# Four edits of order in a perceiver layer: scores and values, a weight load, a norm factor, a bank

## The chip, the cores and the metric

The kernel runs on one core of a Trainium2 chip. The metric is the device time of one execution in microseconds (us), as the median of several runs. The profile is one execution recorded by the hardware profiler.

## What is computed

One layer takes x of 256 tokens by 512 and a context of 4096 tokens by 512, all in 32-bit floats, and adds three blocks to x, each on a layernorm of it:

```python
x = x + _L0_xattn_ref(_layernorm(x), ctx_2048, ...)   # attention
x = x + _L0_attn_ref(_layernorm(x), ...)              # state-space block
x = x + _L0_ffn_ref(_layernorm(x), ...)               # mixture of experts
```

The attention has 16 query heads and 4 key heads of 128, RMS norms on queries and keys, a causal part over the tokens themselves and a full part over the context. The state-space block projects its input, runs a causal convolution of length 4, mixes tokens in two chunks of 128 with decays exp(A_cs[i] - A_cs[j]) of running sums per head, carries a state from the first chunk to the second, gates with silu(z), normalizes and projects back. The mixture routes each token to 6 of 32 experts of width 192, weighs their results, and adds a shared expert of width 384.

## The kernel before

Tokens lie in two tiles of 128 (t = 0, 1). The program is written in plain Python, and a planner fixes the order on each engine: it simulates the program with times of its own and takes, of what is ready on an engine, what stands earlier in the program. Every engine then works strictly in that order and waits on semaphores. `tc.issue_after(ins)` adds an edge: what is traced inside comes behind `ins` on the same engine. DMAs are issued by SP (`nc.sync`), by ACT (`nc.scalar`) and by POOL (`nc.gpsimd`), each a queue in order.

**Attention** (`bounded_attention`). Step s = 0 takes the tokens' own keys, steps 1 to NC = 8 one chunk of 512 context keys each. A step is a list of pieces (s, g, t, i): key head g, token tile t, key block i; 12 pieces in step 0, 32 in the others. For each piece `scores` (L567) is a matmul into one of three `sc` banks, ACT takes exp of it (L573) into one of four `prT` tiles, and DVE multiplies the block on the diagonal by a mask (L576) or adds the probabilities up (L583). `values` (L592) multiplies them by the values into `oT`. The program issues the values of a piece two pieces after its scores (`pending`). Beside steps 1 to 7 run the products of the next chunk's keys and values (`fast_steps`, L364), whose keys are transposed by DVE and through DRAM (`turn_heads`: `kd<-tr` L263, `kT<-kd` L265), as are most queries in step 0 (`qT<-qd`). In the last step the key blocks come in the order 1, 3, 2, 0.

**State-space block.** It begins inside the last step. `decays(t)` brings the running sums to all partitions: ACT writes them to DRAM (L844), POOL loads them 128-fold into `lm`, 1 MB (L845); DVE subtracts each head's own sum (L849, 16 instructions) and ACT takes exp (L850, 4). `channels` projects and convolves (L864 to L873), `gates` computes silu(z) (L885), `mixing` multiplies `lm` by the products of B and C (L910), `assemble` gates y (L952 to L962), `turn_y` transposes it (L971, L972) and `mamba_out` projects it back (L978), adds it to x (L979) and calls `layernorm`, whose factor is a power on POOL (`power_half`, L196); L206 then writes xn.

**Mixture.** `route`, `ranks`, `rows_of` give each token's experts and rows (L1004 to L1077). `scatter(t)` issues 6 indirect DMAs from POOL (L1022) that write xn to the experts' rows in DRAM. `shared_hidden` and `shared_down` (L1135 to L1149) are the shared expert. `hold` gives the experts' weights, two experts a pair, the buffers that have come free, and loads the first pairs from SP (L1165, L1166); the later pairs are gathered by POOL (L1158). `Rounds` then runs the pairs of experts: the rows of the first two pairs are picked by a matmul (`ps_pick`, L1466, copied by DVE and ACT at L1468), the others fetched from DRAM.

**Banks of PSUM.** There are 8: `ps_tp` 1, `ps_mm` 2, `ps_sc` 3, `ps_o` 2. `bank(name)` takes the next of a ring over `mm`, `sc` and `tp`. Before `Rounds` these pools close and others take over the banks: `ps_x` 2, `ps_gu` 2, `ps_t` 1, `ps_ye` 3; the first matmul into a bank waits until what lay there has been read.

Of the kernel before, what the change touches and what calls it, by code (L numbers as in the profile page):

```python
# [19 lines left out]
P = 128  # L20
# [53 lines left out]
def perceiver_layer(ctx: ExitStack, tc: tile.TileContext, a: dict, out: bass.AP):  # L74
# [65 lines left out]
    def layer(ctx, bounded):  # L140
# [410 lines left out]
        def bounded_attention(beside):  # L551

            pp = pool("pp", 4)
            bq = small.tile([P, 3], FP, tag="bq", name="bq", bufs=1)
            V.tensor_reduce(bq[:, 0:1], qw_bc, AX.X, ALU.max, apply_absolute_value=True)
            V.tensor_reduce(bq[:, 1:2], kw_bc, AX.X, ALU.max, apply_absolute_value=True)
            shift = bq[:, 2:3]
            V.tensor_scalar(shift, bq[:, 0:1], bq[:, 1:2], -float(np.sqrt(HD)), ALU.mult, ALU.mult)
            V.tensor_scalar(shift, shift, BOUND, None, ALU.add)
            outs, first_pr, masked = {}, [], []  # L560

            def scores(s, g, t, n):

                kT, _, r = kv[s]
                i = keys_of(s, t)[n]
                sc = ps_sc.tile([P, REP * P], FP, tag="sc", name="scT")
                TE.matmul(sc, kT[:, g, i * P:(i + 1) * P], qT[:, t, heads4(g), :].rearrange("p h q -> p (h q)"),  # L567
                          start=True, stop=True)
                la = lacc[:, t, g, :]

                alone = s == 0 and t == 0
                pr = la if alone else pp.tile([P, REP * P], FP, tag="pr", name="prT")
                S.activation(pr, sc, AF.Exp, bias=shift, scale=SCALE if r is None else r[:, i, g:g + 1])  # L573
                if s == 0 and i == t:
                    p3 = pr.rearrange("p (h q) -> p h q", q=P)
                    masked.append(V.tensor_tensor(p3, p3, upper.unsqueeze(1).to_broadcast([P, REP, P]), ALU.mult).ins)  # L576
                if s == 0:
                    if n < t:
                        first_pr.append(pr)
                    elif not alone:  # L580
                        V.tensor_tensor(la, first_pr.pop(), pr, ALU.add)
                else:
                    V.tensor_tensor(la, la, pr, ALU.add)  # L583
                return pr

            def values(s, g, t, n, pr):
                _, v, _ = kv[s]
                keys = keys_of(s, t)
                i, last = keys[n], n == len(keys) - 1
                if n == 0:  # L590
                    outs[g, t] = ps_o.tile([P, REP * P], FP, tag="o", name="oT")
                TE.matmul(outs[g, t], v[:, i, g * HD:(g + 1) * HD], pr, start=(n == 0), stop=last)  # L592
                if last:
                    ov = oacc[:, t, g, :]
                    if s == 0:
                        V.tensor_copy(ov, outs.pop((g, t)))
                    else:
                        V.tensor_tensor(ov, outs.pop((g, t)), ov, ALU.add)  # L598
                    if s == NC:
                        ps = ps_sc.tile([P, REP * P], FP, tag="sc", name="ps_l")  # L600
                        TE.matmul(ps, ones, lacc[:, t, g, :], start=True, stop=True)
                        rl = lacc[:, t, g, :]
                        V.reciprocal(rl, ps)  # L603
                        V.tensor_tensor(aT[:, t, heads4(g), :].rearrange("p h q -> p (h q)"), ov, rl, ALU.mult)

            pending = []
            for s in range(NC + 1):
                if s < NC:
                    steps = [(s, g, t, i) for g in range(NKV) for t in range(NT) for i in range(len(keys_of(s, t)))]
                else:  # L610
                    steps = [(s, g, t, i) for t in range(NT) for g in range(NKV) for i in range(len(keys_of(s, t)))]
                    last_weights()
                extra = []
                if 0 < s < NC:
                    if s + 1 < NC:
                        load_ctx(s + 1)
                    extra = fast_steps(s, heads_done[4] if s == 1 else None)
                    extra.insert(len(extra) // 2, lambda: clear(s - 1))
                done = 0
                for n, st in enumerate(steps):  # L620
                    if s == 0 and n == 3:
                        for turn in turns:
                            turn()
                    if s == 0 and n == 8:
                        with tc.issue_after(masked[-1]):
                            last_sum()
                    pending.append((*st, scores(*st)))
                    if s == 0 and st[3] == len(keys_of(s, st[2])) - 1:
                        q = qT[:, st[2], heads4(st[1]), :]
                        S.activation(q, q, AF.Copy, scale=kw_col)  # L630
                    if len(pending) > 2:
                        values(*pending.pop(0))
                    if s < NC:

                        while done < min(len(extra), len(extra) * (n + 1) // (len(steps) - 4)):
                            extra[done]()
                            done += 1
                    elif n > len(steps) // NT + 1:
                        for f in beside():
                            f()  # L640
            for p in pending:
                values(*p)
# [151 lines left out]
        def steps_of(t):  # L794
# [37 lines left out]
                    S.activation(m["e1", t], acs, AF.Exp)  # L832
            return product, series, sums

        def decays(t):


            lm, acs = m["lm"], m["acs", t]

            def spread_sums():  # L840
                ps = bank("ps_csT")[0:SH, 0:P]
                TE.matmul(ps, m["dA", t], upper, start=True, stop=True)
                S.copy(m["csT", t], ps)
                S.dma_start(sums_d[t], m["csT", t])  # L844
                G.dma_start(lm, sums_d[t].partition_broadcast(P))  # L845

            def piece(q):
                for hh in range(q * 4, q * 4 + 4):
                    V.tensor_scalar(lm[:, hh, :], lm[:, hh, :], acs[:, hh:hh + 1], 0.0, ALU.subtract, ALU.min)  # L849
                S.activation(lm[:, q * 4:q * 4 + 4, :], lm[:, q * 4:q * 4 + 4, :], AF.Exp)  # L850
            return [spread_sums] + [lambda q=q: piece(q) for q in range(4)]

# [122 lines left out]
        def mamba_out(t):  # L975
            ps = bank("ps_out")
            for k in range(DIT):
                TE.matmul(ps, m["yT", t][:, k, :], w_out[k // 4][:, k % 4, :], start=(k == 0), stop=(k == DIT - 1))  # L978
            V.scalar_tensor_tensor(x_sb[:, t, :], ps, m["ry", t], x_sb[:, t, :], ALU.mult, ALU.add)  # L979
            layernorm(t)  # L980


        def routing_memory():
# [32 lines left out]
                            m["idx"][:, t, 0:TOPK].unsqueeze(2).to_broadcast([P, TOPK, NE]), ALU.is_equal)  # L1016
            V.tensor_reduce(m["mask"][:, t, :], m["hot"][:, t].rearrange("p k e -> p e k"), AX.X, ALU.add)

        def scatter(t):

            for k in range(TOPK):
                G.indirect_dma_start(  # L1022
                    out=xg_rows[t * TOPK + k], in_=xn[:, t, :], in_offset=None,
                    out_offset=bass.IndirectOffsetOnAxis(ap=row[:, t, k:k + 1], axis=0))
# [118 lines left out]
            return product, turn  # L1143

        def shared_down(t):
            ps = bank("ps_shared")
            for j in range(FT):
                TE.matmul(ps, m["act"][:, j, tok(t)], sd[:, j, :], start=(j == 0), stop=(j == FT - 1))
            V.tensor_tensor(x_sb[:, t, :], ps, x_sb[:, t, :], ALU.add)  # L1149
# [8 lines left out]
            G.indirect_dma_start(out=out, out_offset=None, in_=src,  # L1158
                                 in_offset=bass.IndirectOffsetOnAxis(ap=place[:, c:c + 1], axis=0))

        def load_weights(to, n, fixed):

            if fixed:
                for i in range(2):
                    nc.sync.dma_start(to[i], a["experts"][2 * n + i])  # L1165
                nc.sync.dma_start(to[2], a["down_rest"][2 * n:2 * n + 2].rearrange("e p n -> (e p) n"))  # L1166
            else:
                s = 2 * n - FIXED
# [1 line left out]
                    rows_at(to[i], a["experts"].rearrange("e p n -> (e p) n"), s + i)  # L1170
                rows_at(to[2], a["down_rest"].rearrange("e p n -> (e p) n"), NE - FIXED + s // 2)

        def load_pair(n):
            if n < NP:
                k = n % NHELD
                weights[n] = (held[2 * k], held[2 * k + 1], rests[k])
                load_weights(weights[n], n, 2 * n < FIXED)

        def hold(*tiles):

            for tl in tiles:
                held.append(carve(tl, (WEX,))[0])
                if len(held) % 2 == 0 and len(held) <= FIXED:
                    load_pair(len(held) // 2 - 1)


        run = lambda fs: [f() for f in fs]
# [51 lines left out]
        sums()  # L1239
        lm[0]()  # L1240
        run(chans[1][c] for c in order[3:])
        hold(*w_x, lacc[:, 0])
        run(gates(0))
        run(lm[1:])
        assemble(0)
        silu[1]()
        run(tokens_back(1))
# [15 lines left out]
        ranks(0)  # L1263
        rows_of(0)
        product, turn = shared_hidden(0)
        mamba_out(1)
        product()
        scatter(0)
        hold(wvc, wkc, ctx0)
        hold(*w_out)  # L1270
        pick = pick.rearrange("p (t e) r -> p t e r", t=NT)
# [366 lines left out]
```

## Time and profile before

| | us |
|---|---|
| median of 3 runs (996.19, 996.37, 998.72) | 996.37 |
| the profiled execution | 998.33 |
| its span, first to last instruction | 996.6 |
| PE busy | 970.6 |
| DVE busy | 499.3 |
| ACT busy | 386.2 |
| POOL busy | 204.8 |
| mean granted clock of PE | 0.996 |

The time of the profiled execution holds its span and 1.7 us around it. PE is TensorE, DVE VectorE, ACT ScalarE, POOL GpSimd and SP the engine that issues DMAs. A matmul of 32-bit floats is recorded as two instructions, 0.43 us apart at 512 columns, so a score or a value takes PE 0.86 us. Times in the views count from the start of the span; a name such as `oT<-prT,v` is what an instruction writes and reads.

### The profile page before, as it was taken

The numbers are of one execution on the slowest core, as the hardware profiler recorded it, in microseconds if no ns is written. First come the engines' busy times: TensorE is split into PE (matmuls) and PEld (weight loads), VectorE is DVE, ScalarE is ACT, GpSimd is POOL, SyncE is SP. The second block draws the span as 40 slices with busy tenths as digits, with TensorE's granted clock in tenths as the row PEclk, the third lists the DMA queues.
The fourth block names the chain that finished last, engine by engine and source line by source line (L and its number), as shares of the span: only waits on it lengthen the run. The fifth ranks groups of instructions, "written<-read, shape, count | busy, mean of one in ns | idle before, by whom it ended". The sixth has DMA issues, their size and how long they took to land.

```text
span 996.6 us, 8898 instructions
## 1 busy us (share of the span) xinstructions
PE 970.6 (97%) x2742; PEld 456.7 (46%) x2742; DVE 499.3 (50%) x999; ACT 386.2 (39%) x851; POOL 204.8 (21%) x212
## 2 busy tenths in 40 slices
PE   7999999999999999999999999999999898999996
PEld 3444444444444444444444444444466554555442
DVE  4456554454453544544545545458596655422134
ACT  3645543443443443434434434343162821122210
POOL 4443001101100201200200200000013324444533
PEclk9999999999999999999999999999999999999998
DMA  8735032213313304304304113140054542899964
GB/s 318 230 74 150 21 97 95 62 33 115 85 21 127 84 6 142 85 0 148 74 11 148 34 32 83 56 115 1 1 183 169 211 177 109 316 343 352 393 231 121
DMA packets 131580, 125.91 MB, mean 126 GB/s; under 512 B 80225, under 2 KB 99586, under 8 KB 126274
## 3 DMA queue, kind: packets, MB, share of 16 engines
q1 hardware_dynamic: 119216, 77.96, 25.9%
q0 software_dynamic: 7984, 41.16, 11.1%
q10 hardware_dynamic: 4322, 6.11, 1.7%
q8 instruction: 24, 0.39, 0.2%
q14 instruction: 34, 0.28, 0.1%
HBM read 89.02 MB, written 36.19 MB: 126 GB/s over the span
## 4 chain that ended last, share of the span: by engine, by line
PE 94%; DMA 2%; DVE 1%; ACT 1%; issue 1%; POOL 1%; SPq 0%; ACTq 0%; DVEq 0%
PE oT L592 23%; PE scT L567 23%; PE ps_kv L364 17%; PE ps_egu L218 5%; PE ps_self L218 3%; PE ps_v L218 2%; PE ps_o L788 2%; PE ps_egu L1373 2%; PE total L1441 2%; PE ps_ye L1450 2%; PE ps_k L218 1%; PE ps_out L978 1%; PE ps_xbc L218 1%; PE xgTp L1354 1%; PE ps_ye L1453 1%; DMA lm<-sums 1%
## 5 line engine op out<-in xcount | busy, mean ns | idle before, releaser
L583 DVE TENSOR_TENSOR lacc<-lacc,prT 128x512 f32<-128x512 f32 x256 | 182.7, 714 | 240.4 <-ACT prT L573 239.6
L573 ACT ACTIVATE prT<-scT,bq,rk 128x512 f32<-128x512 f32 x256 | 198.8, 777 | 255.4 <-PE scT L567 242.7
L567 PE MATMUL scT<-qT,kT 128*128 128x512 f32 x536 | 270.9, 592 | 0.0
L592 PE MATMUL oT<-prT,v 128*128 128x512 f32 x528 | 268.0, 592 | 0.9 <-ACT prT L573 0.9
L592 PEld LDWEIGHTS oT<-prT,v 128*128 128x128 f32 x528 | 100.1, 190 | 127.2 <-issue 115.0
L567 PEld LDWEIGHTS scT<-qT,kT 128*128 128x128 f32 x536 | 101.2, 190 | 124.6 <-issue 121.9
L196 POOL TENSOR_TENSOR rk<-pv,mhalf 128x4 f32<-128x4 f32 x32 | 32.3, 1009 | 371.1 <-DVE pv L195 371.1
L364 PE MATMUL ps_kv<-wkv,fast 128*128 128x512 f32 x112 | 53.4, 592 | 0.0
L254 ACT ACTIVATE sq<-kraw 128x128 f32<-128x128 f32 x128 | 35.7, 279 | 45.2 <-DVE kraw L382 43.2
L364 PE MATMUL ps_kv<-wkv,ctx 128*128 128x512 f32 x112 | 52.8, 592 | 0.0
L364 PE MATMUL ps_kv<-fast,fast 128*128 128x512 f32 x112 | 52.6, 592 | 0.0
L598 DVE TENSOR_TENSOR oacc<-oT,oacc 128x512 f32<-128x512 f32 x64 | 43.7, 682 | 0.0
L364 PEld LDWEIGHTS ps_kv<-wkv,fast 128*128 128x128 f32 x112 | 21.3, 190 | 26.8 <-issue 26.8
L364 PEld LDWEIGHTS ps_kv<-wkv,ctx 128*128 128x128 f32 x112 | 21.3, 190 | 26.8 <-issue 23.7
L364 PEld LDWEIGHTS ps_kv<-fast,fast 128*128 128x128 f32 x112 | 21.3, 190 | 26.8 <-issue 21.8
L358 POOL TENSOR_TENSOR fast<-ctx 128x512 f32<-128x512 f32 x7 | 9.3, 1334 | 113.1 <-PE ps_kv L364 94.2
L382 DVE TENSOR_TENSOR kraw<-ps_kv,fast 128x256 f32<-128x256 f32 x42 | 17.9, 425 | 28.2 <-PE ps_kv L364 28.2
L1425 DVE TENSOR_TENSOR hid<-si,ps_egu 128x128 f32<-128x128 f32 x18 | 5.2, 287 | 53.3 <-ACT si L1423 53.3
L788 PE MATMUL ps_o<-wo,qT 128*128 128x512 f32 x64 | 28.8, 592 | 0.0
L218 PE MATMUL ps_self<-wq,xT 128*128 128x512 f32 x64 | 28.1, 592 | 0.0
L603 DVE RECIPROCAL lacc<-ps_l 128x512 f32<-128x512 f32 x8 | 26.8, 3346 | 0.1
L364 PE MATMUL ps_kv<-fast,ctx 128*128 128x512 f32 x56 | 26.3, 592 | 0.0
(392 smaller groups left out, 1131.6 us busy)
## 6 DMA issues: line engine op xcount, KB each, us to landing
xg<-xn SPq DMA_DIRECT2D x6, 2560.0 KB
ctx<-in_ctxT_dram SPq DMA_DIRECT2D x7, 1024.0 KB
kd<-tr SPq DMA_DIRECT2D x112, 64.0 KB
kT<-kd SPq DMA_DIRECT2D x28, 256.0 KB
ye<-y_sb ACTq DMA_DIRECT2D x22, 256.0 KB
wq<-in_wq_dram SPq DMA_DIRECT2D x4, 1024.0 KB
wo<-in_wo_dram SPq DMA_DIRECT2D x4, 1024.0 KB
w_in<-in_W_inT_dram SPq DMA_DIRECT2D x4, 1024.0 KB
```

Of the source, the lines that this page charges most:

```text
L196: return G.tensor_tensor(dst, v[:, :n], mhalf[:, :n], ALU.pow)
L218: TE.matmul(ps, lhs(k), rhs_of(k), start=(k == 0), stop=(k == KD - 1))
L254: S.activation(sq[:, h, :], raw[:, h, :], AF.Square, accum_out=ss[:, h:h + 1])
L364: TE.matmul(ps, lhs(k), rhs(k), start=(start and k == 0), stop=(k == 1), skip_group_check=True)
L567: TE.matmul(sc, kT[:, g, i * P:(i + 1) * P], qT[:, t, heads4(g), :].rearrange("p h q -> p (h q)"), start=True, stop=True)
L573: S.activation(pr, sc, AF.Exp, bias=shift, scale=SCALE if r is None else r[:, i, g:g + 1])
L583: V.tensor_tensor(la, la, pr, ALU.add)
L592: TE.matmul(outs[g, t], v[:, i, g * HD:(g + 1) * HD], pr, start=(n == 0), stop=last)
L598: V.tensor_tensor(ov, outs.pop((g, t)), ov, ALU.add)
L603: V.reciprocal(rl, ps)
L788: TE.matmul(m["ps_o", t], aT[:, t, h, :], wo[j][:, h % 4, :], start=(h == 0), stop=(h == NH - 1))
L1373: TE.matmul(ps[self.half(i)], xT[:, k, self.half(i)], w[i][:, k, :], start=(k == 0), stop=(k == KD - 1))
```

## The change

Nothing is computed otherwise, and no instruction is added or removed. Four edits change an order or a bank:

1. In step 0, and in the first four pieces of the last step, the values issued after a piece's scores get an edge behind those scores.
2. `hold(*w_x, lacc[:, 0])`, which loads the first pair of experts, moves behind `gates(0)` and the decays, and its two loads of 1 MB wait for the first DVE instruction of the decays of tile 1 (L849), which reads `lm`.
3. `scatter(0)` is cut into 2 and 4 indirect DMAs; the 4 stand behind the norm factor of `layernorm(1)` on POOL.
4. `shared_down(1)` takes a bank of `ps_o` in place of the ring's next.

```diff
+                scored.append(TE.matmul(sc, kT[:, g, i * P:(i + 1) * P], qT[:, t, heads4(g), :].rearrange("p h q -> p (h q)"),
+                                        start=True, stop=True).ins)
...
                     if len(pending) > 2:
-                        values(*pending.pop(0))
+                        with tc.issue_after(scored[-1]) if s == 0 or (s == NC and n < 4) else nullcontext():
+                            values(*pending.pop(0))
...
-                    V.tensor_scalar(lm[:, hh, :], lm[:, hh, :], acs[:, hh:hh + 1], 0.0, ALU.subtract, ALU.min)
+                    begun = V.tensor_scalar(lm[:, hh, :], lm[:, hh, :], acs[:, hh:hh + 1], 0.0, ALU.subtract, ALU.min)
+                    if hh == 0:
+                        decay_begun.append(begun)
...
-            layernorm(t)
+            return layernorm(t)
...
-        def scatter(t):
-            for k in range(TOPK):
+        def scatter(t, ks=range(TOPK)):
+            for k in ks:
...
-            ps = bank("ps_shared")
+            ps = bank("ps_shared") if t == 0 else ps_o.tile([P, REP * P], FP, tag="o", name="ps_shared")
...
+        def wait_for(dma, behind):
+            if behind is not None:
+                tc.add_manual_dep(dma.ins, behind.ins.name, mybir.DependencyInfo(
+                    mybir.DependencyClass.Sync, mybir.DependencyReason.DATA), reason="transfers in order")
...
-                    nc.sync.dma_start(to[i], a["experts"][2 * n + i])
+                    wait_for(nc.sync.dma_start(to[i], a["experts"][2 * n + i]), behind)
...
-        hold(*w_x, lacc[:, 0])
         run(gates(0))
         run(lm[1:])
+        hold(*w_x, lacc[:, 0], behind=decay_begun[-1])
...
-        mamba_out(1)
+        normed = mamba_out(1)
         product()
-        scatter(0)
+        scatter(0, range(2))
+        with tc.issue_after(normed.ins):
+            scatter(0, range(2, TOPK))
```

## The prediction

> **What bounds the kernel now.** I read the page first, then the waits of TensorE, then the chain of waits, and last the timeline around each wait.
>
> ```profile
> span 996.6 us, 8898 instructions
> PE 970.6 (97%) x2742; PEld 456.7 (46%) x2742; DVE 499.3 (50%) x999; ACT 386.2 (39%) x851; POOL 204.8 (21%) x212
> ```
>
> TensorE (PE) is busy for 970.6 of 996.6 us, and the change neither adds nor removes a matmul. Only the 26.0 us in which PE is idle can shrink: 6.3 us wait for the first weights and 7.7 us lie behind the last matmul (it ends at 988.87). Of the rest, the waits of PE from 60 us on are, the longest first:
>
> ```profile
> PE ps_pick L1466 <- DVE x_sb L1149: 1.9, 1, 1.9
> PE ps_out L978 <- DVE qT L972: 1.8, 1, 1.8
> PE ps_sh L1141 <- DVE sh L1136: 1.6, 1, 1.6
> PE oT L592 <- DVE lacc L576: 1.5, 1, 1.5
> PE oT L592 <- ACT prT L573: 0.9, 1, 0.9
> ```
>
> Each is one wait, and each part of the change touches one or two. The two `oT` waits sit at 98.10 us (step 0) and 662.35 us (last step). The chain of waits shows how the 1.8 us at `ps_out` arise:
>
> ```profile
> 777.52 9.31 DMA lm<-sums
> 786.90 1.28 ACT L850
> 788.19 0.63 ACT lm L850
> 788.84 1.28 ACT L885
> 790.13 0.60 ACT wkv L885
> 790.75 1.28 ACT L850
> 792.04 0.64 ACT lm L850
> 792.71 0.69 DVE lm L910
> 793.40 0.61 DVE qT L972
> 794.05 7.13 PE ps_out L978 x16
> ```
>
> The columns are start, length and what ran. The transfer of the running sums (9.31 us) is followed by ScalarE (ACT), which loads a table (1.28 us) at each turn between exp and silu. The windows around `ps_pick` show a second loss:
>
> ```profile
> 842.44:844.30 1.86, 0.00 (x1) 0.00 (x1) 1.70 (x8) 0.00 (x0) 1.55 (x2) 1.00 0.68 262
> 844.30:848.00 3.70, 3.70 (x5) 1.65 (x6) 1.82 (x11) 0.00 (x0) 2.79 (x4) 0.54 0.49 189
> ```
>
> After 1.86 us without a matmul the granted clock (third number from the end) is 0.54 over 3.70 us. That stretch loses 3.70 x 0.46 = 1.70 us. It counts as busy time.
>
> **Part 1, values behind scores.** In step 0 PE runs the scores of piece 6 at 95.58, then at once the values of piece 6, which need exp (0.69) and mask (0.69); hence 1.50 us of wait. With the edge, values 4, 5 and the scores 7, 8 come between: 4 x 0.86 = 3.44 us of work covers the chain. The price would be a score that waits for its query. The last query transfer is issued at 88.38 and its bytes are over by 91.5 us; score 7 then comes at about 95.5, 4 us later. Gain 1.5 us, bounds 0 and 1.6.
> In the last step PE runs three values at 657.84 (2.58 us) while the fourth key block is in flight (issued 657.49, bytes from 658.5 to 660.0), takes its score at 660.41 and waits 0.92 us for its exp. With the edges the second value stands behind that score. If other scores fill the time, 0.92 us are gained. If none does, PE waits from 658.70 to about 660.2, 1.5 us, and saves 0.92 + 0.25 of the old order, so it loses 0.3. Between the ends I take 0.5, nearer to the gain, since the next group's scores need neither that block nor a new query.
>
> **Part 2, weights behind the sums.** Two experts' weights (1 MB each, SP, 777.32) and `lm` (1 MB, POOL, 777.52) share the DMA engines. Between 777 and 782 the hardware queue moves 1.02 MB and POOL's queue 0.25. The same transfer for the other tile, issued at 734.96 with nothing beside it, had its bytes between 736.0 and 739.1, 4.1 us after issue. Alone, `lm` lands at 781.7 instead of 786.8; VectorE (DVE) is ready at 782.50 and drops its 4.35 us wait. What is late next is ACT: its silu ends at 785.85, so its table load moves from 786.90 only to 785.87. The five ACT steps behind it, 5.8 us, stay, then L910 and L972 follow: `ps_out` starts 1.0 us earlier, 0.8 us still waited. Bounds: 0 (next paragraph) and 1.77. The held loads now start at about 783; behind them on SP stand the loads of `lacc` (782.81) and later ones, first read from 858 on, the held ones from 852.97: 60 us of cover, without which 2 MB would cost 5 us.
> The row: POOL's transfer was issued at 777.52 and its bytes came late, while DVE ran short f32 products without a break (777.09 to 782.50). The Trainium skill, "SBUF — State Buffer", section "SBUF: two separate sides", says that a DVE operation holding the shared port keeps GpSimd from writing descriptors, so that such a transfer seems blocked. By that rule the weights are not the cause, and part 2 would be worth 0.0 us instead of 1.0; the transfer of the other tile, 4.1 us with DVE 4.42 of 4.54 us busy, speaks against it.
>
> **Part 3, a norm factor between scatters.** The timeline around 825 us (start, length, engine, line, operation; in brackets the idle time before and what ended it):
>
> ```profile
> 824.03 0.96 POOL L1022 DMA_INDIRECT xg<-xn,row  x1 [0.30 <-issue]
> 825.01 0.59 POOL L196 TENSOR_TENSOR rs<-pv,mhalf 128x1 f32<-128x1 f32 x1
> 825.63 0.61 DVE L206 TENSOR_SCALAR xn<-x_sb,mv,rs 128x512 f32<-128x512 f32 x1 [3.04 <-issue]
> 826.16 0.54 DVE L1136 TENSOR_TENSOR sh<-sh,ps_sgu 128x384 f32<-128x384 f32 x1
> 826.76 0.55 PE L1141 MATMUL ps_sh<-ident,sh 128*128 128x128 f32 x3 [1.64 <-DVE sh L1136]
> ```
>
> The factor's input is ready at 822.6 us, but POOL first issues four scatters (1.27 us each); DVE stands 3.04 us on L206, and L1136 behind it. With two scatters ahead POOL is free at 822.46, the factor is done at 823.4, L206 at 824.05. L1136 then waits for the last `ps_sgu` matmul (825.12) and PE goes on at about 825.8, not 826.76: 1.0 us. Bounds 0.3 (L206 late by half a scatter) and 1.64 (the transposes of xn fill the gap). The four scatters behind end 0.4 us later (828.5 for 828.08); the next on POOL comes at 838.40, so that costs nothing; without that cover, 0.4.
>
> **Part 4, another bank.** `ps_pick` waits for L1149 to read `ps_shared` (844.24), whose bank it takes over. In a bank of `ps_o` that read is off the path: `ps_pick` may start at 842.44. Of the 1.86 us, DVE can take back 1.0: its queue is full until 846.22, the copy of the first quarter stands there, and the third quarter (842.44 + 2 x 1.72 = 845.9) needs that bank, free at 846.9. Bounds 0.86 and 1.86; I take 1.4. The half-rate stretch, 1.7 us, should go with the wait.
> Row: 1.86 us without a matmul, then 3.4 us at half rate. The Trainium skill, "TensorE: Matmul & The Clock Gate", section "What's actually happening", says that the clock falls after an idle window of about 3.4 us, and that windows run free of the kernel. By it so short a wait is not the cause, and the stretch would stay, with a profile at 992.9 in place of 991.2; the trace's length agrees with the window, its cause not.
>
> **Sum.** 1.5 + 0.5 + 1.0 + 1.0 + 1.4 = 5.4 us, 7.1 with the clock. The profiled execution took 998.33 (span 996.6 and 1.7 around it); the runs' median is 996.37, 1.96 lower. That is about the 1.7 us of the stretch, so I take it that the two faster runs had none. Profile: 998.33 - 7.1 = 991.2. Median: 996.37 - 5.4 = 991.0. Behind 853 us PE is busy throughout and carries the gain to the end: the last weights are in at about 957.5 and used at 973, so an earlier PE meets no DMA. I forecast 991.1.
>
> **Rivals.**
> A. The waits form again in the queues of DVE and ACT: last step -0.3, part 2 nothing, part 4 0.86, first step 1.5, part 3 0.3. That gives 2.4 us, 994.0. For it: ACT and DVE are the late ones in three of five places. Chance 0.12.
> B. POOL's descriptors, not the weights, delay `lm`, and the unheld `lacc` load (782.81) then collides with its tail. Part 2 is 0: 992.1. Chance 0.13.
> C. The median too had a half-rate stretch, which goes: 996.37 - 7.1 = 989.3. For it: one profile cannot tell. Chance 0.08.
> D. The emitted order hardly changes, since it is the planner's: 996.4. Against: the edges name exactly the pairs that waited. Chance 0.04.
> E. Slower. The planner orders all of PE anew behind step 0. If it sets a value straight behind its own score at each of the seven step boundaries, as it did at 98.10 and 662.35, each costs 0.92 to 1.50 us; at 1.3 that is 9.1 us against 5.4 gained, 1000.1. It decides above 1.2 us each. Against: the edges bind steps 0 and 8 alone, and between 120 and 570 us PE shows no wait. Chance 0.09.
>
> **Numbers.** The forecast has 0.54, with 988.6 to 993.4 as its own range. A measurement of this kernel tells 0.3%, 3.0 us, from no change. Faster by more: forecast, B and C, 0.75. Same: A and D, 0.16. Slower: E, 0.09. The range runs from 988.0 (C and the better bounds) to 995.2 (past A); outside lie D, E and some 0.05 of the edges.
>
> **What would show it.** No wait of `oT` on L576 or L573; a first L849 of the second tile at about 782.5 and `ps_out` waiting about 0.8 us; L196 behind two scatters and `ps_sh` waiting about 0.7; `ps_pick` with no wait on L1149 and granted clock 1.00 there. I am wrong if PE shows new waits between 100 and 650 us, if L849 still waits for `lm`, or if `ps_pick` loses its 1.86 us to L1468.

## The result, and the profile after

Four runs of the changed kernel took 988.99 to 990.28 us, median 989.48; four of the kernel before beside them 996.19 to 999.59, median 997.55. The ratio is 0.9918 (95% interval 0.9896 to 0.9940). A later set gave 989.53 against 997.2, ratio 0.9929 (0.9915 to 0.9942). So the change saves 7 to 8 us. The forecast of 991.1 was near, and the side was right. But the median it started from was too low, and it left the clock out of the median: two wrong steps that offset each other in part. Three of its five gains were also larger than told.

The profiled execution took 989.35 us, its span 987.6. The head of the page and the waits of TensorE (PE) from 60 us on (in total, times, longest; in us):

```profile
span 987.6 us, 8901 instructions
PE 968.4 (98%) x2742; PEld 456.0 (46%) x2742; DVE 497.8 (50%) x999; ACT 386.5 (39%) x851; POOL 206.0 (21%) x212
```

```profile
PE total L1457 <- DVE hidS L1428: 1.0, 1, 1.0
PE ps_dt L218 <- DVE xT L213: 0.8, 1, 0.8
PE ps_out L984 <- DVE qT L978: 0.7, 1, 0.7
PE ps_z L218 <- ACT xc L871: 0.7, 1, 0.7
PE ps_sh L1147 <- DVE sh L1142: 0.7, 1, 0.7
```

The 3 instructions more than before are semaphore operations of PE's and ScalarE's (ACT's) sequencers, which compute nothing. Line numbers are up to 16 higher than before. Both `oT` waits and the wait of `ps_pick` are gone; those at `ps_out` and `ps_sh` are down to 0.7. PE's busy time fell too, by 2.2 us, though it does the same work: 1.7 us of that is the stretch at half rate in the traced execution of before.

I took the start of the same matmul in both traces, milestone by milestone. What an edit gained is the step in the difference:

| stretch | milestones, us before and after | gained, us |
|---|---|---|
| first weights (not the change) | `lnT` 19.46, 18.64 | 0.82 |
| step 0 | last `oT` 105.50, 102.85 | 1.83 |
| last step | first `ps_l` 666.75, 663.09 | 1.01 |
| weights behind the sums | `ps_out` 794.05, 789.38 | 1.02 |
| norm factor | `ps_sh` 826.76, 821.16 | 0.92 |
| bank | `ps_pick` 844.30, 836.68 | 2.02 |
| clock at `ps_pick` | `ps_egu` 852.97, 843.60 | 1.75 |

Between these rows the difference stays constant to 0.02 us, over the seven context steps too. Later 0.2 us are lost at `total`, and the spans differ by 9.0. The timeline of after around the two shortened waits (start, length, engine, line, operation; in brackets the idle time before and what ended it), first `ps_out` at 789.38:

```profile
778.89 3.57 DVE L853 TENSOR_SCALAR lm<-lm,xc 128x128 f32<-128x128 f32 x16
788.03 0.69 DVE L916 TENSOR_TENSOR lm<-lm,gu 128x512 f32<-128x512 f32 x1 [1.25 <-ACT lm L856]
788.64 0.68 DVE L978 TENSOR_TENSOR qT<-yTp,by_channel 128x512 f32<-128x512 f32 x1
...
784.16 1.28 ACT L891 ACT_TABLE_LOAD   x1
785.45 0.60 ACT L891 ACTIVATE wkv<-ps_z 128x512 f32<-128x512 f32 x1
786.07 1.28 ACT L856 ACT_TABLE_LOAD   x1
787.37 1.67 ACT L856 ACTIVATE lm<-lm 128x512 f32<-128x512 f32 x3
```

VectorE (DVE) begins the decays with no idle time in brackets: `lm` lands 5.0 us after its issue, just as DVE is ready, and DVE loses 0.04 us. Now `ps_sh`:

```profile
816.80 0.98 POOL L1028 DMA_INDIRECT xg<-xn,row  x1 [0.30 <-issue]
818.01 0.57 POOL L196 TENSOR_TENSOR rs<-pv,mhalf 128x1 f32<-128x1 f32 x1 [0.22 <-DVE pv L195]
...
818.61 0.55 DVE L206 TENSOR_SCALAR xn<-x_sb,mv,rs 128x512 f32<-128x512 f32 x1 [0.69 <-POOL rs L196]
820.55 0.55 DVE L1142 TENSOR_TENSOR sh<-sh,ps_sgu 128x384 f32<-128x384 f32 x1 [1.40 <-PE ps_sgu L218]
...
821.16 0.55 PE L1147 MATMUL ps_sh<-ident,sh 128*128 128x128 f32 x3 [0.72 <-DVE sh L1142]
```

The factor comes behind the second scatter, L206 no longer delays L1142, and L1142 waits for PE's own `ps_sgu`, as forecast. At `ps_pick` the window of after (length; busy time of PE, its weight loads, DVE, ACT, POOL, with counts; granted clock; DMA share; GB/s) shows PE busy throughout at full rate:

```profile
836.07:843.17 7.10, 7.10 (x17) 2.96 (x16) 6.70 (x33) 0.59 (x1) 5.27 (x7) 1.00 0.51 194
```

### The profile page after: what moved, and what is told of

It is laid out like the page before. It is cut to its first block, busy times and chain, and to the rows that moved or that the text cites. A ratio compares the mean times of both kernels' runs of the same rounds, so it can differ in the third digit from the quotient of the medians.

```text
span 987.6 us, 8901 instructions
## 1 busy us (share of the span) xinstructions
PE 968.4 (98%) x2742; PEld 456.0 (46%) x2742; DVE 497.8 (50%) x999; ACT 386.5 (39%) x851; POOL 206.0 (21%) x212
## 4 chain that ended last, share of the span: by engine, by line
PE 94%; DMA 2%; DVE 1%; ACT 1%; POOL 1%; issue 1%; SPq 0%; POOLq 0%; DVEq 0%
PE scT L567 23%; PE oT L592 23%; PE ps_kv L364 17%; PE ps_egu L218 5%; PE ps_self L218 3%; PE ps_v L218 2%; PE ps_o L790 2%; PE ps_ye L1466 2%; PE ps_xbc L218 1%; PE ps_out L984 1%; PE ps_egu L1389 1%; PE ps_k L218 1%; PE ps_sgu L218 1%; PE total L1457 1%; PE xgTp L1370 1%; PE ps_ye L1469 1%
```

## Experiments

**The kernel before, again.** No edit.

> The kernel before, unchanged, to read span and granted clock run by run. My base (runs near 996.3 had no half-rate stretch, runs near 998.5 had one): runs in two groups about 1.7 us apart, the faster with a mean granted clock of about 0.998, the slower 0.996. Rival (every run has the stretch ahead of ps_pick, and the scatter comes from elsewhere, such as the wait for the first weights): all runs at 0.996, with spans that differ at one clock.

Twelve runs, 995.71 to 1000.62 us, median 997.09, in one broad group, at granted clocks from 0.995 to 0.999. Neither expectation held. The trace shows two things by which executions of one kernel differ. Its waits of PE:

```profile
PE ps_pick L1466 <- DVE x_sb L1149: 1.9, 1, 1.9
PE ps_sh L1141 <- DVE sh L1136: 1.6, 1, 1.6
PE oT L592 <- DVE lacc L576: 1.5, 1, 1.5
PE oT L592 <- ACT prT L573: 0.9, 1, 0.9
PE ps_dt L218 <- DVE xT L213: 0.8, 1, 0.8
PE ps_out L978 <- DVE qT L972: 0.8, 1, 0.8
```

`ps_out` waits 0.8 us, not 1.8, with no edit made; and the clock stays at 1.00 behind the same wait of `ps_pick`. Both are taken up below.

**The bank alone.**

```diff
-            ps = bank("ps_shared")
+            ps = bank("ps_shared") if t == 0 else ps_o.tile([P, REP * P], FP, tag="o", name="ps_shared")
```

> Edit 4 alone (the bank of ps_o). If its worth is what the two traces show, ps_pick no longer waits for the read of ps_shared (1.9 us before), starts about 2.0 us earlier, and the half-rate stretch of 1.75 us behind it is gone: 3.7 us of span against a profile of the kernel before that has the stretch, granted clock 0.998. Rival (the stretch comes at a time of its own, by the Trainium skill's free windows): the wait is gone, 2.0 us, but a stretch of about 3.4 us at half rate stays somewhere near. Rival (L1468 on VectorE takes it back): 0.9 to 1.0 us.

Ratio 0.9982 (0.9971 to 0.9992), 995.42 us. The wait is gone, `ps_pick` comes 2.02 us earlier against the milestone ahead of it, and no stretch follows. DVE takes nothing back: its copy of the first quarter moved forward in its queue. That the stretch is gone proves nothing here, since it was missing in the run before, too.

**Work in the wait of `ps_pick`.**

```diff
+            if t == 1:
+                with tc.issue_after(last.ins):
+                    busy = ps_o.tile([P, REP * P], FP, tag="o", name="ps_busy")
+                    for j in range(2):
+                        TE.matmul(busy, xn[:, 0, 0:P], xn[:, 0, :], start=(j == 0), stop=(j == 1))
```

> The kernel before with two added matmuls, 1.72 us in full precision, into a free bank of ps_o between the last ps_shared matmul and ps_pick; their result is read by nobody. The wait of ps_pick for L1149 stays, but PE works in nearly all of it. If the idle time causes the half rate: no stretch behind it, clock 1.00 at ps_pick, and the span is about 1.7 us shorter than a profile of the kernel before, although PE has 1.72 us more work. If the stretch comes at a time of its own: it stays, and the span is that of before (within 0.3 us).

Ratio 0.9996 (0.9986 to 1.0006). The trace has no stretch, with `ps_pick` at its old place. Without the edit the stretch is missing in some executions as well, so this run decides nothing by itself.

**Step 0 alone.** The edge only where `s == 0`.

> Edit 1 in step 0 alone. By the traces: the 1.5 us wait of oT on L576 is gone, the milestones behind step 0 come 1.8 us earlier than in before (after taking off what the start-up differs), and this holds to the end, with the waits of 1.8 (ps_out), 1.6 (ps_sh) and 1.9 us (ps_pick) as before. Rival E of the prediction (the planner sets values behind their own scores at later step boundaries): new waits of 0.9 to 1.5 us between 100 and 650 us. On the clock: the wait of 1.9 us ahead of ps_pick now comes 1.8 us earlier; if idle time causes the half rate the stretch of 3.4 us follows it again, if it has a time of its own it need not.

Ratio 0.9993 (0.9980 to 1.0006). The trace gains 1.83 us in step 0, and none of it is lost in the context steps: rival E is out. Here the stretch stands behind the 1.7 us wait of `ps_sh`, not behind the 1.9 us of `ps_pick`. This led to the rule for the clock. In every trace each time at one rate, up to the half rate in which the trace ends, is a whole number of 3.413 us (832.85 us in before is 244 of them, 976.21 is 286), whatever the kernel does: the clock is set anew at the borders of windows that run on their own. Two windows from each of three kernels, the traced before, the run again, and step 0 alone (columns as above):

```profile
840.97:844.38 3.41, 1.55 (x7) 0.69 (x6) 2.80 (x17) 0.00 (x0) 2.80 (x3) 1.00 0.60 231
844.38:847.79 3.41, 3.41 (x4) 1.38 (x5) 1.74 (x11) 0.00 (x0) 2.50 (x4) 0.50 0.45 174
```

```profile
839.75:843.16 3.41, 2.81 (x9) 1.00 (x7) 2.67 (x18) 0.00 (x0) 2.80 (x3) 1.00 0.39 153
843.16:846.57 3.41, 2.15 (x5) 1.06 (x6) 3.12 (x17) 0.00 (x0) 2.50 (x4) 1.00 0.48 185
```

```profile
821.09:824.50 3.41, 1.62 (x10) 1.04 (x9) 1.48 (x3) 0.83 (x2) 2.80 (x4) 1.00 0.45 173
824.50:827.91 3.41, 3.41 (x5) 1.35 (x4) 0.28 (x1) 0.93 (x1) 0.00 (x0) 0.50 0.20 77
```

Where PE is busy for 1.55 or 1.62 of 3.41 us, the next window runs at 0.50. In the run again the border cut the same wait in two (2.81 and 2.15 busy), and nothing happened.

**The weights alone.** The wait of the two loads on L849 and the place of `hold`, without the rest.

> Edit 2 alone (the weights behind the running sums). Five traces of kernels that load the weights early show two cases: lm lands 9.3 to 9.9 us after its issue and ps_out waits 1.8 to 1.9 us, or it lands after 7.2 to 8.1 us and ps_out waits 0.7 to 0.8. Theory (the edit takes away the bad case and nothing more, because ScalarE's table loads set the 0.75 us): lm lands about 5.0 us after issue, ps_out waits 0.7 to 0.8 us, and the median falls by 1.0 us times the share of bad cases, 0.3 to 0.6 us, hardly measurable. The prediction's own step: 1.0 us in every run. Rival B (POOL's descriptors delay lm while VectorE works): lm still takes 7 us or more.

Ratio 1.0005 (0.9996 to 1.0014): no gain in the median. `lm` was there 5.0 us after its issue and `ps_out` waited 0.8. Rival B is out: DVE was as busy as before, and only the weights had moved. Over all traces, the time from the issue of `lm` to the first decay that reads it, and the wait of `ps_out`:

| | issue to first decay, us | wait, us |
|---|---|---|
| weights early, 3 traces | 9.3, 9.7, 9.9 | 1.8 to 1.9 |
| weights early, 4 traces | 7.0, 7.1, 7.2, 8.2 | 0.7 to 0.8 |
| weights held back, 7 traces | 4.7 to 5.3 | 0.6 to 0.8 |

The edit takes away 2 to 5 us of transfer. In time it is worth what `lm` takes beyond about 8.3 us: from `ps_l` to `ps_out` the traces with 7.0 to 8.2 us lose nothing, and those with 9.3, 9.7 and 9.9 us lose 1.0, 1.4 and 1.6 us.

**The last step and the norm factor.** Edit 1 where `s == NC and n < 4`, and edit 3.

> Edits 1 in the last step and 3, without the others: places 160 us apart, read separately in the trace. Theory: between the milestones ahead of the last step and ps_l 1.0 us are gained, with no wait of oT on L573 and no new wait; between ps_out and the first ps_sh 0.9 us, ps_sh waiting 0.7 (without a half-rate stretch between). The prediction's sizes: 0.5 and 1.0. Clock theory (windows of 3.41 us, free of the kernel; a window in which PE is idle for more than about half sets the next to half rate): the 1.9 us wait ahead of ps_pick is followed by a stretch only if it lies within one window.

Ratio 0.9990 (0.9974 to 1.0006). The last step gains 1.19 us and the factor 0.92. Behind `ps_pick`'s wait a stretch follows, after a window with PE busy for 1.51 of 3.42 us.

**The changed kernel, again.** No edit to it.

> The changed kernel once more, beside the same runs of before as the parts. Sum of the parts by the traces: 1.83 (step 0) + 1.01 (last step) + 0.92 (factor) + 2.02 (bank) = 5.8 us that every run gains, 0 to 1.0 from the weights by run, and what the half-rate stretches cost the runs of before (1.7 us each, in some runs none, in some more than one): 7 to 8 us between the medians, ratio 0.992 to 0.993. If only the forecast's 5.4 held: 0.9946. Its trace shows no window with PE idle for more than half between 20 and 975 us, and so no stretch.

Ratio 0.9929, as told. Six runs, 988.87 to 990.98 us, all at granted clocks of 0.997 or 0.998; the trace has no stretch and no window below 0.7 busy between 20 and 975 us.

**Three edits more.** The core of each (an edge that sets the fourth product of `lm` behind the copies L978 is not shown):

```diff
+                with tc.issue_after(gated[-1]) if gated and t else nullcontext():
                     S.activation(lm[:, q * 4:q * 4 + 4, :], lm[:, q * 4:q * 4 + 4, :], AF.Exp)
...
-                    add(got, 0)
+                    late = got
+                    add(late, 0, range(TOPK - 1))
...
                     spread_last(n)
+                    if n == LAST + 1:
+                        with tc.issue_after(main.done[n]):
+                            add(late, 0, [TOPK - 1])
...
+        for i in range(5):
+            TE.matmul(warm[:, 0:P], ones, ones, start=True, stop=True)
```

> The changed kernel and three edits more. (a) The exps of the decays of tile 1 stand behind both silus of gates(0) on ScalarE (one table load in place of three), and the fourth lm product behind both copies of yTp on VectorE: if table loads set the remaining 0.75 us at ps_out, the wait goes or falls below 0.2; if it is VectorE's queue or TensorE, it stays. (b) The last x_sb add of tile 0 stands behind the hidS copy: the 1.0 us wait of total on hidS goes; or it forms again at the next hidS. (c) Nine matmuls of 128 columns on a constant, read by nobody, run while TensorE waits for its first weights: if the clock rises at the end of a window of 3.41 us in which PE is busy for about 0.85 or more, the full rate begins at 4 to 8 us in place of 8.7 to 13.7, and lnT comes at about 18.6, where the loads of the first weights bind; if the clock counts something else, it begins where it did. Together 1.7 us less than the changed kernel from (a) and (b) and 0 to 2 from (c): ratio to before about 0.989 to 0.991.

Ratio 0.9927 (0.9914 to 0.9941), 989.38 us: no better than the changed kernel. (a) The four exps now follow each other and end at 787.1 in place of 789.0, yet `ps_out` still waits 0.6: table loads were worth 0.13 us. What is left is short: transposes `yTp`, one copy (0.68) and the matmul that reads it. (b) The wait of `total` is gone, and PE ends at 978.04 instead of 979.70. The span ends only 0.6 us earlier, as POOL's last step of 6.59 us begins 1.5 us behind PE's end, in the nine traces before this one 0.1 to 0.9; why, I did not find. (c) The start (timeline):

```profile
1.21 2.50 PE L143 MATMUL warm<-ones 128*128 128x128 f32 x10 [1.21 <-POOL ones L115]
3.69 2.07 PE L239 MATMUL warm<-ones 128*128 128x128 f32 x8
5.55 2.10 PE L223 MATMUL ps_k<-wkv,ctx 128*128 128x512 f32 x4
9.54 2.72 PE L223 MATMUL ps_k<-wkv,ctx 128*128 128x512 f32 x5 [1.89 <-DMA wkv<-in_wk_ctx_dram]
```

The full rate begins at 5.76 us, in the others at 8.7 to 14.5. PE then overtakes the loads and waits 1.89 us; `lnT` comes at 18.53, hardly ahead of the best starts without it. The clock is no better for it: (1 - clock) x span averages 3.29 us over the six runs, with 2.14 for the changed kernel. About 0.5 us of that is no loss: in its trace 9.0 us in place of 7.9 lie behind PE's end, and the clock ends at half rate there. Whether the new wait of 1.89 us, more than half of a window, brings the half rate back in some runs is not shown; in the trace it did not.

**The bank undone.** The changed kernel with `bank("ps_shared")` for both tiles.

> The changed kernel with edit 4 undone: ps_pick takes over the ring's bank again and waits 1.9 us for L1156 to read ps_shared. It is the only place where PE can be idle for more than half of a window of 3.41 us. Window theory: sliding such windows over the traces, a window that holds more than half of the wait exists at 0.54 of all phases, so of the runs about half cost 2.0 us (989.5 + 2.0 = 991.5, granted clock 0.998) and half 3.7 us (993.2, clock 0.996), the median between. Theory of the prediction (each such wait is followed by the stretch): all runs near 993.2. Theory of no link: all near 991.5.

Ratio 0.9956 (0.9940 to 0.9972), against 0.9929 for the changed kernel in its own set, with intervals that just meet: by these two, edit 4 is worth 2.7 us in this surrounding. The theories can't be judged by the median of 994.09: they were told in us, and the kernel before, beside these runs, took 998.48 and not 997.2. The seven runs have clocks of 0.995 to 0.999, three at 0.996 or less, where the changed kernel had none.

**The bank undone, its wait filled.** The same two matmuls as above.

> As the run before, with two added matmuls (1.72 us, read by nobody) in the wait of ps_pick. The wait for the read stays, PE is busy in it. Window theory: no run has a stretch, all near 991.5 with clock 0.998, so the added work makes the median about 0.9 us shorter than without it. Theory of no link between idle time and clock: the same runs as without the added work.

Ratio 0.9949 (0.9931 to 0.9968). By the medians the two can't be told apart. By the clock they can be set side by side: (1 - clock) x span, averaged over the runs, is 2.84 us (standard error 0.59) with the wait and 1.98 (0.36) with the wait filled; the changed kernel has 2.14 (0.16), in its traces all behind PE's end, where the clock falls in every trace. The clock is recorded to 0.001, which is 1 us of a run. None of the six is at 0.996 or less. With the eleven runs of the same kernel in the last experiment, the 18 runs with the wait average 3.03 (0.27), so the difference is 1.05 (0.45): on the side of the window theory, though six runs are few.

**The weights undone.** The changed kernel without edit 2.

> The changed kernel with edit 2 undone: the first two weights are loaded early again. In the traces with the early load, lm took 7.0 to 8.1 us (ps_out waits 0.7) or 9.3 to 9.9 us (ps_out waits 1.8). Theory: the runs lie between 989.5 and 992.2: nothing lost in the first case, 1.0 us in the second, and another 1.7 us where the window about ps_out then is idle for more than half (about 0.55 of those). Median 989.7 to 990.7. The prediction's step (1.0 us in every run): all at 990.5 or above.

Ratio 0.9947 (0.9928 to 0.9966), 1.8 us above the changed kernel's, with intervals that overlap. In its trace `lm` took 9.7 us and `ps_out` waited 1.9. The runs' median is 993.4 and not 990.5, but the set is not comparable in us: the kernel before had 998.48 in it, and all three traces of the set show ScalarE (ACT) late at the first `si`, with up to 1.5 us of wait at `hidTp` behind it.

**The bank undone, again.**

> The changed kernel with edit 4 undone, once more, for two things left open. In the first trace of it ScalarE began its first si (L1439) 2.8 us after the matmuls it reads, with no releaser in the trace, and PE waited 0.4 us at hidTp; the first traces of the other two kernels of that set showed the same with 1.0 and 1.5 us. If it belongs to this kernel's order, it is there again; if it belongs to the chip or the run, it is gone. And the window theory again: the trace shows a half-rate stretch of 3.41 us behind ps_pick if, and only if, the window ahead of it has PE idle for more than half; about half of the runs have granted clock 0.996 or less, where the changed kernel has 0.997 to 0.999.

Ratio 0.9960 (0.9947 to 0.9973), 992.28 against 996.44 us. The late `si` is gone, so it does not belong to this kernel. This trace has the stretch, and the window ahead of it:

```profile
835.43:838.84 3.41, 1.68 (x7) 0.81 (x6) 2.65 (x17) 0.00 (x0) 2.68 (x3) 1.00 0.54 210
838.84:842.25 3.41, 3.29 (x4) 1.51 (x5) 1.91 (x12) 0.00 (x0) 2.50 (x4) 0.50 0.45 174
```

Same kernel as three experiments earlier, same wait, other border. Three of the eleven runs have a clock of 0.996 or less; with the first experiment's it is 6 of 18, fewer than the half that was expected.

## Why the prediction was right, and where it was not

**Step 0 and last step: right, undersized.** 1.83 for 1.5 (bounds 0 to 1.6) and 1.01 for 0.5. The term that failed is the wait taken at its listed length. In the timeline of before the matmul after the listed 1.50 us starts 2.10 us after its predecessor, where 0.43 is usual, and the next one 0.53 after that: 1.67 + 0.10 = 1.77. Matmuls overlap (0.59 long, 0.43 apart), so a wait also costs the 0.16 us of overlap and 0.10 of restart. The profile models the ends of matmuls, so the 0.16 us may lie in the listing of a wait and not in PE. The same 0.26 lifts 0.92 to the 1.19 seen without the other edits. In the first trace of the changed kernel the last step pays 0.17 of it at the key block, which comes just late; in the second it gains the full 1.19. The doubt that made me take 0.5 was worth that much, in some executions.

**Weights: the cause right, the size right for one execution alone.** The weights did delay `lm`, DVE dropped its wait, 0.75 us remained and 1.0 was gained against the traced run. The 4.1 us that I took for `lm` alone was short (5.0 measured), which cost nothing, as DVE was ready no sooner. But I took one execution for all. In four of seven traces with the weights early, nothing is lost at `ps_out`; the other three lose 1.0, 1.4 and 1.6 us, so the mean worth is about 4.0/7 = 0.6 us. The step "table loads bound what is left" fell: without two of them 0.6 us remain, and 0.13 us were gained.

**Norm factor: right.** 0.92 for 1.0, and the 0.7 us left at `ps_sh`. No wait shows behind the four later scatters in either trace of the changed kernel.

**Bank: right, undersized.** 2.02 for 1.4; of the two ends the upper one held, with the overlap of 0.16 on top.

**The clock: wrong.** I tied the stretch to the wait and then left it out of the median, because two of three runs were about 1.7 us faster. A wait of 1.9 us meets a window's border or doesn't. Sliding windows of 3.413 us over the busy times of PE and counting those with more than half idle gives, for the traces of before, 0.8 stretches a run with an early `lm` and 1.3 with a late one; for the changed kernel none. Measured over runs, the loss (1 - clock) x span is 3.33 us on average before (23 runs) and 2.14 after (6 runs): 1.2 us (standard error 0.3), or 0.7 stretches of 1.71 us.

The Trainium skill, "TensorE: Matmul & The Clock Gate", section "What's actually happening", says that windows run free of the kernel, and the traces agree (3.413 us). By the Trainium skill's rule of an idle window there, though, 1.86 us of idle time would not do. Here, between the start and PE's last window, each window with 1.5 to 1.7 us busy was followed by half rate (one in each of five traces), and none with 1.78 us or more was. The border is not sharp in these records: with the bank undone and its wait filled, PE's last window was busy for 1.49 us and the next still ran at the full rate. So the stretch depends on where the borders fall, which no edit sets, and the change, which leaves no window that idle, takes the chance away. That idle time causes it rests on these five windows and on the comparison of clocks with the wait filled (1.05 us, standard error 0.45); no single run proves it. This is rival C in part: its mechanism at 0.7 of its size.

**The sum.** The base failed as well: the three runs' 996.37 was low, the larger sets have 997.2 and 997.3 (two later ones 998.48 and 996.44, so only the ratio within a set is compared). Spans averaged over runs fell from 995.74 to 987.98, 7.8 us: 1.2 by the clock and 6.6 by waits. The traces give 1.83 + 1.01 + 0.6 + 0.92 + 2.02 = 6.4 for the waits. The forecast had 5.4 and no clock, from a base 0.8 too low: 991.1, where 989.5 was measured. What stays open: the medians of the single edits add up to about 3 us, less than the 7 of the whole. The clock may explain a part: the runs with step 0 alone and with the weights alone lost 4.1 and 3.9 us by it (standard errors 0.3), those of before 3.2 and 3.3. Both keep the waits of `ps_sh` and `ps_pick`, but before has them too, and why they lost more is not shown.

**Rivals.** A is out: none of the five waits formed again at its full length, and ACT and DVE took nothing back at `ps_pick`. B is out by the weights alone. D is out by the milestones, E by the constant difference from 105 to 657 us. What I missed is the wait at `total` behind `hidS`, 0.8 us before and 1.0 after; I had called PE busy throughout behind 853.

## What to carry to other kernels

Here a wait of PE cost 0.16 to 0.33 us more than its listed length where it went whole (`oT` and `ps_pick`), and 1.7 us more in executions where it filled over half of a window of the clock, so look at how much idle time lies close together, not at single waits. One profile is one execution: before a transfer's delay or a clock stretch is priced, look whether it is there in a second one. And take out such waits together: while one is left that can fill half of a window, some executions still pay for a stretch.

## What the hardware showed that I had not expected

Between the start and PE's last window the clock fell after each window with PE at most 0.49 busy (0.44, 0.46, 0.48, 0.48, 0.49) and held at 0.52 and more; one last window of 0.44 held too. At the start it took more to raise it: it rose after windows busy for 0.88 to 1.0, and not after 0.22 to 0.88. Where that border falls sets when the full rate begins, 8.7 to 14.5 us into the span, and with it where `lnT` comes, from 18.6 to 20.7 us: 2 us of scatter between executions that no edit of order touches.

One 1 MB transfer between the same two places took 7.0 to 9.9 us beside two others of its size, and 4.7 to 5.3 without them, up to the first instruction that read it. Its first packets came 3.8 to 3.9 us after its issue in all seven traces beside them and 1.4 in all seven without: the late start was the same each time, and what differed from run to run was the transfer behind it.
